# Operands' taps and steps on three rotating PSUM banks, and the last image's 3x3 convolution by pairs of rows

## The chip, the cores and the metric

The kernel runs on one core of one Trainium2 chip, in one launch. The metric is the device time of an execution in microseconds (us); smaller is better. The engines are named as in the profile: PE is TensorE, whose weight loads are shown as PEld, DVE is VectorE, ACT is ScalarE, POOL is GpSimd, SP is SyncE. SP issues almost all DMA transfers, in the order in which its instructions stand.

## The reference

The input is x, 4 images of 128 channels by 64x64 pixels, in f32. Four layers follow each other, each with a residual and each behind a group norm `gn` of 32 groups:

```python
x = x + attention(gn(x), Wq, bq, Wk, bk, Wv, bv)   # 4096 tokens of 128 channels, softmax(q k / sqrt(128)) v
x = x + conv5x5(gn(x), radial kernel of 5x5 taps)
x = x + scan_layer(gn(x), ...)                     # see below
x = x + conv3x3(gn(x), main_w) + main_b
```

The scan layer applies a 1x1 convolution, and splits the 128 channels into two halves, of which the second runs over the pixels backwards. Each half gets a causal convolution of 4 taps and a silu (the result is `xt`), then `delta = softplus(xt @ Wd + bd)`, `Bm = xt @ WB` and `Cm = xt @ WC`, and for every channel and each of 64 states the recurrence

```python
h[t] = exp(delta[t] * A) * h[t-1] + delta[t] * xt[t] * Bm[t]
y[t] = sum over the states of h[t] * Cm[t] + D * xt[t]
```

A 1x1 convolution leads back to 128 channels. The other branch of the 3x3 layer's `where` gives the same value, so that only the 3x3 convolution itself is computed.

## The kernel before

**Three streams in one order of instructions.** An image is a tile of 128 channels by 4096 pixels in SBUF. A PSUM bank holds 128x512 f32, so that an image is 8 tiles of 512 pixels or 4 chunks of 1024 (16 rows of 64 pixels). The Python generators `images`, `front`, `attention_start`, `conv_pairs`, `scan_operands` and `back` emit instructions piece by piece, and the loop at the end of `program` interleaves them with `scan_core`, the recurrence. `scan_core` has 1024 ticks, 256 for each image; the image number is b. A tick is one pass over 128 rows (32 channels times 4 states) of 1024 pixels: a decay on ACT (L1075), a drive `db` on POOL (L1082), the scan on DVE (L1092), the product with Cm on DVE (L1095) or on POOL (L1113), and the sum over the states on PE (L1127). Each engine executes what it is given in that order. While the ticks of image b run, `front` works on image b+1: attention, the 5x5 convolution by pairs of rows (`conv_pairs`), then the operands of its own scan.

**The operands.** `scan_operands` makes delta, delta*xt, Bm and Cm of an image for `scan_core`. It walks in slots; tile i (0 to 7) starts at slot 5i. The steps of tile i, with their slots counted from its start, are

| slot | step | engine, line |
|---|---|---|
| 0, 1 | `taps`: 8 matmuls of half width (4 taps, two directions) into the bank `pt` | PE L887 |
| 4 | `halves`: half of `pt` to SBUF (`xc`), its tanh (for b > 0 in place, in `pt`) | ACT L901, L906 |
| 5 | `silu`: product of the two, into `xc` | DVE L910 |
| 8 | `delta_product`: matmul into the bank `pz` | PE L919 |
| 9, 12 | `row_product` of Bm and of Cm, both through the bank "a" | PE L919 |
| 10, 12 | `softplus`, `exp` on `pz` | ACT L932, L933, L959, L964 |
| 11, 13 | `row`: the two rows to SBUF, and from there to DRAM | ACT L924, SP L926 |
| 13 | `digits`: reads `pz` for the last time | DVE L938, L939 |

So PE meets, in each five slots, `taps(k)`, the second `row_product(k-2)`, `delta_product(k-1)`, the first `row_product(k-1)`, and then `taps(k+1)`. After tiles 3 and 7 (1, 5 and 7 in image 0) come the logarithms (ACT L968, with a table load before and after), `join` and `drives` on POOL (L944, L949) and the writes of delta and delta*xt. Before the first ticks of image b are emitted, `before(b)` draws out work until the first chunk of its operands is ready. `load` then brings the operands from DRAM for the ticks (L1052, L1058), on the SP queue.

All `pt` of an image use one bank, "s". A tile `pt(k+1)` can be written only when `pt(k)` has been read for the last time: by `silu(k)` for b > 0, by `halves(k)` for b = 0. The `pz` alternate between the banks "z" and "s2". The bank pool that holds "s2" is closed when the last image's operands are done, and its space becomes two double-width tiles "da" (`widen`).

**The end.** After the last tick, `scan_end` and `group_norm` of image 3 run, and then `back(3)`, with nothing beside it. It calls `conv` (from L610 on): ACT writes the normalised image into a padded tile in four pieces (L370), and for each of the 8 tiles of 512 pixels PE accumulates 9 products (L644), one for each tap. `put` adds bias and image on DVE (L1278), and SP writes the tile out (L1279). For images 0 to 2 the image is added by a tenth matmul with the identity, and the tile leaves over ACT; that work lies among the ticks of image 3.

`program(True)` is a second version of everything, for inputs whose softmax leaves the safe range; it is not entered here. It reads its convolution weights back from the DRAM copy `kept`.

Of the kernel before, what the change touches and what calls it, by code (L numbers as in the profile page):

```python
# [24 lines left out]
F32 = mybir.dt.float32  # L25
I32 = mybir.dt.int32
AF = mybir.ActivationFunctionType
ALU = mybir.AluOpType
# [4 lines left out]
P = 128  # L33
GROUPS = 32
GN_EPS = 1e-5
CH = 1024
MM = 512
# [8 lines left out]
PRODUCT, HOP, SLOT, PACE, ENDPACE, AHEAD = 0.86, 1.7, 0.7, 2.8, 1.5, 4  # L46


BQ, BK, BX, BP, CONVB, BD, DSKIP, MAINB, CONVW, ALOG = 0, 1, 2, 3, 4, 5, 6, 7, 8, 12
# [3 lines left out]
def conv_preact_kernel(  # L53
# [16 lines left out]
    nc = tc.nc  # L70
    B, C, H, W = x.shape
    L = H * W
    NCH = L // CH
# [6 lines left out]
    NM = L // MM  # L80
# [4 lines left out]
    of = out.rearrange("b c h w -> b c (h w)")  # L85
# [3 lines left out]
    dram = ctx.enter_context(tc.tile_pool(name="dram", bufs=2, space=DRAM))  # L89
    ps = ctx.enter_context(tc.tile_pool(name="ps", bufs=1, space=PSUM))  # L90
    pools, ready = {}, set()
    more = None

    def bank(tag, name):
        return pools.get(tag, ps).tile([P, MM], F32, tag=tag, name=name)
# [32 lines left out]
    def col(i):  # L128
        return vec[:, i : i + 1]
# [93 lines left out]
    cw = const.tile([P, NTAP + 10, C], F32, name="cw")  # L223
    taps5 = cw[:, :NTAP, :]

    m3 = cw[:, : main_w.shape[1], :]
    kept = dram.tile([P, main_w.shape[1], C], F32, tag="kept", bufs=1, name="kept")

    def build_conv_weights(tmp):
        xx_sb = tmp.tile([P, NTAP, C], F32, name="xx_sb")  # L230
        nc.sync.dma_start(xx_sb, xhat)
        id_sb = tmp.tile([P, C], F32, name="id_sb")
        nc.sync.dma_start(id_sb, identity)
        picked = tmp.tile([P, 2, NTAP, C // 2], F32, name="picked")
        for n, (which, table, inds) in enumerate((("xx", wxx, indsxx), ("id", wid, indsid))):
            nr, oc = table.shape[1], table.shape[2]
            acc = picked[:, n]
            one = cw.rearrange("p k c -> p (k c)")[:, : NTAP * oc]
            one = one.rearrange("p (k o) -> p k o", o=oc)
            tab = tmp.tile([P, nr, oc], F32, name=f"tab{which}")  # L240
            nc.sync.dma_start(tab, table)
            ii = tmp.tile([P, NTAP], I32, name=f"ii{which}")
            nc.sync.dma_start(ii, inds.to_broadcast([P, NTAP]))
            fi = tmp.tile([P, NTAP], F32, name=f"fi{which}")
            nc.vector.tensor_copy(fi, ii)

            ng = tmp.tile([P, NTAP], F32, name=f"ng{which}")
            nc.vector.tensor_scalar(ng, fi, 0.0, float(nr), ALU.is_lt, ALU.mult)
            nc.vector.tensor_tensor(fi, fi, ng, ALU.add)
            nc.vector.tensor_scalar(fi, fi, 0.0, float(nr - 1), ALU.max, ALU.min)  # L250
            for r in range(nr):
                hit = tmp.tile([P, NTAP], F32, name=f"hit{which}{r}")
                nc.vector.tensor_scalar(hit, fi, float(r), None, ALU.is_equal)
                hit_b = hit.unsqueeze(2).to_broadcast([P, NTAP, oc])
                tab_b = tab[:, r : r + 1, :].to_broadcast([P, NTAP, oc])
                if r == 0:
                    nc.vector.tensor_tensor(acc, tab_b, hit_b, ALU.mult)
                else:
                    nc.vector.tensor_tensor(one, tab_b, hit_b, ALU.mult)
                    nc.vector.tensor_tensor(acc, acc, one, ALU.add)  # L260
                yield HOP

        for t in range(2):
            def every(ap):
                return ap.rearrange("p k (o t) -> p k o t", t=2)[:, :NTAP, :, t]

            idb = id_sb.rearrange("p (o t) -> p o t", t=2)[:, :, t].unsqueeze(1)
            idb = idb.to_broadcast([P, NTAP, C // 2])
            nc.vector.tensor_tensor(every(xx_sb), every(xx_sb), picked[:, 0], ALU.mult)
            nc.vector.tensor_tensor(every(cw), picked[:, 1], idb, ALU.mult)  # L270
            yield HOP
        nc.vector.tensor_tensor(taps5, taps5, xx_sb, ALU.add)
        for n in range(2):
            row = cw[:, (1 + 2 * n) * 5 :]
            nc.vector.tensor_tensor(
                cw[:, NTAP + n * 5 : NTAP + (n + 1) * 5, :], row[:, :5], row[:, 5:10], ALU.add
            )
        nc.sync.dma_start(kept, m3)

# [1 line left out]
    ASIZE, VSIZE = HP * (W + PAD) + PAD, (H + 2) * (W + 2) + PAD  # L283
# [85 lines left out]
    def normalise(dst, src, gn):  # L369
        nc.scalar.activation(dst, src, AF.Identity, scale=gn[0], bias=gn[1])  # L370
# [292 lines left out]

# [198 lines left out]
    def scan_operands(b, xn, mats4, piece):  # L867


        bc, dd, dxd, xcd, xsd = mats4  # L870
        pad = KC - 1

        xc = large(b, f"xc_{b}")[:, :L]
        delta = pools["big"].tile([P, L], F32, tag="xt", name=f"delta_{b}")
        pts, ths, pzs, pbs, us = {}, {}, {}, {}, {}

        def taps(i, *ks):
            if ks[0] == 0:
                pts[i] = bank("s", f"pt_{b}_{i}")
            pt = pts[i]  # L880
            t = i * MM
            for k in ks:
                lo = L + 2 * pad - 1 - k - t - (MM - 1)
                views = (xn[:, t + k : t + k + MM], xn[:, lo : lo + MM][:, ::-1])
                for d, view in enumerate(views):
                    r = slice(d * HALF, (d + 1) * HALF)
                    nc.tensor.matmul(  # L887
                        pt[r, :], wtap[:, k, r], view,
                        start=k == 0, stop=k == KC - 1,
                        tile_position=(0, d * HALF), skip_group_check=True,  # L890
                    )
                    if i == 0 and k == 0:
                        nc.tensor.matmul(
                            pt[r, : pad], ident[:, r], edge, start=False, stop=False,
                            tile_position=(0, d * HALF), skip_group_check=True,
                        )
# [20 lines left out]
        def product(i, m, tag):  # L917
            pb = bank(tag, f"pb{m}_{b}_{i}")
            nc.tensor.matmul(pb, bdiag[:, m, :], xc[:, bass.ts(i, MM)], start=True, stop=True)  # L919
            return pb  # L920
# [29 lines left out]
            nc.sync.dma_start(dxd[c], xc[:, cut])  # L950

        def delta_product(i):
            pzs[i] = product(i, 0, ("z", "s2")[i % 2])

        def row_product(i, m):
            pbs[i, m] = product(i, m, "a")
# [9 lines left out]
        def logs(i, j):  # L966
            for n in range(i, j):
                nc.scalar.activation(us[n], us[n], AF.Ln)  # L968

        slots = {}  # L970

        def at(slot, f, *args):
            slots.setdefault(slot, []).append((f, args))

        EVERY = 5
        for i in range(NM):
            t = EVERY * i
            at(t, taps, i, 0, 1)
# [14 lines left out]
        for i, j in zip(cuts, cuts[1:]):  # L993
            t = EVERY * (j - 1) + 15
            at(t, logs, i, j)
# [203 lines left out]
    def program(safe):  # L1199
# [1 line left out]
        mats4, ynds, ends = {}, {}, {}  # L1201
        ready.clear()
        if safe:
            nc.sync.dma_start(m3, kept)

        def load(tile, b):
            for c in range(NCH):
# [15 lines left out]
        def front(b, xn, v):  # L1223

            xs = large(b + 1, f"xs_{b}")[:, :L]
            st = Sums(f"e{b}")
            yield from attention(b, xs, xn, v, st, safe, load(xs, b))
            st2 = Sums(f"s{b}")

            yield from conv_pairs(b, xs, f"A{b % 2}", st, st2, b > 0 or safe)  # L1230
            if b + 1 == B:
                nc.sync.dma_start(m3, main_w)

            def mat(name):
                return dram.tile([NCH, P, CH], F32, tag=name, name=f"{name}_{b}")

            mats4[b] = (
                [mat("bm"), mat("cm")], mat("dd"), mat("dxd"), mat("xcd"),
                dram.tile([P, L], F32, tag="xsd", bufs=B, name=f"xsd_{b}"),
            )  # L1240
            ynds[b] = dram.tile([NM, P, MM], F32, tag="ynd", bufs=B, name=f"ynd_{b}")
            operands = yield from scan_prep(b, xs, st2, mats4[b])
            if b + 1 < B:
                return (yield from both(operands, start(b + 1, 10)))
            yield from operands

        def stage(b, pieces, done):

# [19 lines left out]
        def back(b):  # L1268
            xs, st, _ = ends[b]

            def put(i, acc):
                cut = bass.ts(i, MM)
                if b + 1 < B:
                    to = pools["bg"].tile([P, MM], F32, tag="w", bufs=4, name=f"o_{b}_{i}")
                    nc.scalar.activation(to, acc, AF.Identity, bias=col(MAINB))
                else:
                    to = xs[:, cut]
                    nc.vector.scalar_tensor_tensor(to, acc, col(MAINB), to, ALU.add, ALU.add)  # L1278
                nc.sync.dma_start(of[b][:, cut], to)  # L1279

            yield from conv(b, xs, "V", st, m3, 3, put, "m", residual=b + 1 < B)

        def both(*gens):

# [174 lines left out]
```

## Time and profile before

| what | us |
|---|---|
| median of 3 runs (4513.7 to 4527.3) | 4513.8 |
| the profiled execution, its own time | 4519.1 |
| its span, first to last instruction | 4517.3 |
| busy in the span: PE | 3996.2 |
| busy: DVE | 3667.9 |
| busy: POOL | 3638.5 |
| busy: ACT | 2399.5 |
| operands of image 0, from the first `taps` to the last | 643.0 to 694.3 |
| operands of image 1, the same | 1585.9 to 1654.8 |
| operands of image 2, the same | 2542.7 to 2617.2 |
| operands of image 3, the same | 3505.5 to 3568.9 |
| the last image's 3x3 convolution, matmuls | 4444.0 to 4508.7 |

Every f32 matmul shows as two records of the profile. "L887" is line 887 of the kernel. In a timeline, the bracket at the end of a row gives the idle time of that engine just before the instruction, and what ended it. Waits are a list of who waited for whom: us in total, how often, and the longest.

### The profile page before, as it was taken

To read this page: it belongs to the slowest core of one execution; us is meant where nothing else is said; L and a number is where in the kernel's file an instruction comes from. 1 tells how busy PE (TensorE), PEld (TensorE's weight loads), DVE (VectorE), ACT (ScalarE), POOL (GpSimd) and SP (SyncE) were. 2 spreads that over 40 slices of the span, in tenths; PEclk is the share of its full clock that TensorE was granted. 3 is DMA by queue.
4 is the path that set the end of the run, shared out by engine and by line. 5 is a ranking of instruction groups with operands and counts; after the bars stand their busy time and mean duration, and the time that the engine had idled before them with its cause. 6 is when DMAs were issued, how large, how long until landed. Compare 5 with 4: busy or idle time off the path is not lost. (4 is left out here: it accounts for less than half of the span.)

```text
span 4517.3 us, 43608 instructions
## 1 busy us (share of the span) xinstructions
PE 3996.2 (88%) x13528; PEld 1482.2 (33%) x13528; DVE 3667.9 (81%) x3643; ACT 2399.5 (53%) x4420; POOL 3638.5 (81%) x1731
## 2 busy tenths in 40 slices
PE   8999998999999979999999879999999658575767
PEld 4444433333333323333333223333333112121212
DVE  4721217999998978999989879999999799999992
ACT  3333227666664476666654566666654654544441
POOL 3433308999998969999989789999999899999992
PEclk9999999999999989999999989999999878697888
DMA  1000016445444565455445555455445565656561
GB/s 63 6 1 1 5 60 229 171 168 180 170 175 157 174 218 196 172 179 174 174 154 177 188 209 176 162 176 177 175 161 182 211 226 203 233 193 231 184 233 48
DMA packets 210582, 719.51 MB, mean 159 GB/s; under 512 B 24864, under 2 KB 25760, under 8 KB 210208
## 3 DMA queue, kind: packets, MB, share of 16 engines
q1 hardware_dynamic: 208736, 715.87, 44.8%
q8 instruction: 109, 1.79, 0.2%
q14 instruction: 137, 1.12, 0.1%
q10 hardware_dynamic: 1600, 0.73, 0.1%
HBM read 649.07 MB, written 67.44 MB: 159 GB/s over the span
## 5 line engine op out<-in xcount | busy, mean ns | idle before, releaser
L1082 POOL TENSOR_TENSOR db<-dx,br 128x1024 f32<-128x1024 f32 x1024 | 2400.0, 2367 | 226.9 <-DMA dx<-dxd 76.7
L1075 ACT ACTIVATE da<-de,a_neg 128x512 f32<-128x512 f32 (+1 forms) x1795 | 1342.1, 751 | 736.0 <-DVE da L1092 444.5
L465 PE MATMUL sc<-r,x 128*128 128x512 f32 x2048 | 1082.5, 611 | 18.3 <-ACT r L434 12.4
L477 PE MATMUL acc<-pt,v 128*128 128x512 f32 x2048 | 1046.5, 593 | 1.6
L1113 POOL TENSOR_TENSOR hc<-hc,cr 128x1024 f32<-128x1024 f32 x406 | 960.1, 2365 | 17.6 <-ACT last L1108 15.1
L471 ACT ACTIVATE pt<-sc 128x512 f32<-128x512 f32 x1024 | 604.4, 590 | 572.4 <-PE sc L465 563.9
L1127 PE MATMUL y<-hc,sel 128*32 128x512 f32 x4096 | 654.2, 650 | 276.6 <-POOL hc L1113 273.5
L1095 DVE TENSOR_TENSOR hc<-da,cr 128x512 f32<-128x512 f32 (+1 forms) x1067 | 828.4, 776 | 68.8 <-issue 1.3
L1092 DVE TENSOR_TENSOR_SCAN da<-da,last,db 128x512 f32<-128x512 f32 (+1 forms) x464 | 728.1, 1569 | 24.1 <-POOL db L1082 17.6
L1092 DVE TENSOR_TENSOR_SCAN da<-da,da,db 128x512 f32<-128x512 f32 x449 | 577.9, 1287 | 14.3 <-ACT da L1075 13.4
L465 PEld LDWEIGHTS sc<-r,x 128*128 128x128 f32 x2048 | 359.1, 190 | 605.0 <-issue 378.4
L477 PEld LDWEIGHTS acc<-pt,v 128*128 128x128 f32 x2048 | 387.5, 190 | 497.2 <-issue 477.9
L1092 DVE TENSOR_TENSOR_SCAN hc<-da,hc,db 128x512 f32<-128x512 f32 x322 | 413.2, 1283 | 61.9 <-ACT da L1075 31.6
L1092 DVE TENSOR_TENSOR_SCAN hc<-da,last,db 128x512 f32<-128x512 f32 (+1 forms) x304 | 455.9, 1500 | 8.4 <-ACT da L1075 4.7
L519 POOL TENSOR_TENSOR sidep<-sidep,pt 128x512 f32<-128x512 f32 x120 | 170.5, 1421 | 279.9 <-ACT pt L471 277.8
L1127 PEld LDWEIGHTS y<-hc,sel 128*32 128x32 f32 x4096 | 94.1, 111 | 732.3 <-POOL hc L1113 363.6
L644 PE MATMUL pcm<-xpm,cw 128*128 128x512 f32 x576 | 291.2, 653 | 30.5 <-ACT xpm L370 30.5
L519 DVE TENSOR_TENSOR sided<-sided,pt 128x512 f32<-128x512 f32 x120 | 96.0, 800 | 227.5 <-ACT pt L471 226.1
L1092 DVE TENSOR_TENSOR_SCAN da<-da,db 128x512 f32<-128x512 f32 (+1 forms) x154 | 231.0, 1500 | 30.9 <-ACT da L1075 16.2
L808 PE MATMUL pe<-df,cw 128*128 128x512 f32 x560 | 255.2, 598 | 0.0
L499 PE MATMUL zp<-pt,ones 128*32 128x512 f32 x1536 | 202.4, 595 | 5.0 <-DVE xs L563 5.0
L1108 ACT COPY last<-da 128x1 f32<-128x1 f32 x469 | 73.1, 156 | 244.3 <-DVE hc L1095 242.5
(209 smaller groups left out, 2743.2 us busy)
## 6 DMA issues: line engine op xcount, KB each, us to landing
br<-bm SPq DMA_DIRECT2D x512, 512.0 KB, 5.2
cr<-cm SPq DMA_DIRECT2D x512, 512.0 KB, 3.9
de<-dd SPq DMA_DIRECT2D x64, 512.0 KB, 4.8
dx<-dxd SPq DMA_DIRECT2D x64, 512.0 KB, 6.2
x<-in_x_dram SPq DMA_DIRECT2D x16, 512.0 KB, 4.6
xs<-in_x_dram SPq DMA_DIRECT2D x16, 512.0 KB, 5.8
xsd<-xs SPq DMA_DIRECT2D x16, 512.0 KB, 5.2
xcd<-xc SPq DMA_DIRECT2D x16, 512.0 KB, 2.7
```

The costliest lines, as they stand in the source:

```text
L465: nc.tensor.matmul(sc, xn[:, bass.ts(j, P)], rq[blk], start=True, stop=True)
L471: nc.scalar.activation(pt, sc, AF.Exp)
L477: nc.tensor.matmul(acc[blk], v[:, j, :], ring[:, u % NRING, :], start=j == 0, stop=j == NJT - 1)
L519: eng.tensor_tensor(s, s, ring[:, u % NRING, :], ALU.add)
L644: nc.tensor.matmul(acc.rearrange("p (r w) -> p r w", w=W), weights[:, t, :], xp[:, y : y + RPM, dx : dx + W], start=t == 0, stop=t == k * ...
L808: nc.tensor.matmul(flat(acc), cw[:, w * K5 + dx, :] if w < HSUM else more[:, w - HSUM, dx, :], view(r, dx), start=k == 1, stop=k == total ...
L1075: nc.scalar.activation(da, rep["de", b, c, d, g][:, bass.ts(h, size)], AF.Exp, scale=a_neg[:, at(i)])
L1082: nc.gpsimd.tensor_tensor(dbs[i], rep["dx", b, c, d, g], rows["b", b, c, d, q], ALU.mult)
L1092: nc.vector.tensor_tensor_scan(h, da, db[:, cut], before, ALU.mult, ALU.add)
L1095: nc.vector.tensor_tensor(hc[:, cut], h, rows["c", b, c, d, q][:, cut], ALU.mult)
L1113: nc.gpsimd.tensor_tensor(hcs[i], hcs[i], rows["c", b, c, d, q], ALU.mult)
L1127: nc.tensor.matmul(y[r : r + SG, :], sel, hcs[i - KG + 1 + gg][:, bass.ts(h, MM)], start=q == 0, stop=False, tile_position=(0, r), skip_gr ...
```

## The change

1. In `scan_operands`, the `pt` and the `pz` of an image are put in one list in the order of their slots (`pt(i)` at 5i, `pz(i)` at 5i + 8), and take the banks "s", "z", "s2" in turn along it. The last `pz` takes "z". The slots and the order of the instructions on every engine stay.
2. The last image's 3x3 convolution becomes `conv_last`. For a pair of output rows it needs the rows d0 to d3; it forms d2-d1 and d3-d1 on POOL and d1+d2 and d0-d2 on DVE (`combine`), multiplies each of the four by three taps, and gets both rows from the four sums. A chunk of 16 rows takes 12 matmuls into four banks (odd chunks the banks s, a, z, y; even chunks the two tiles "da"). The difference part leaves over ACT (`nc.scalar.copy`) and is added and subtracted on POOL; DVE adds the other three parts and the bias. One DMA writes a chunk.
3. `last_weights` makes the six combined taps that this needs, on DVE, when the last image's operands have been emitted. `kept` grows from 9 to 15 taps.

```diff
+    LSUM, LDIF, NKEPT = 9, 12, 15
+    kept = dram.tile([P, NKEPT, C], F32, tag="kept", bufs=1, name="kept")
...
+    def last_weights():
+        half, above = cw[:, LSUM : LSUM + 3, :], cw[:, LDIF : LDIF + 3, :]
+        nc.vector.tensor_tensor(half, m3[:, 0:3, :], m3[:, 6:9, :], ALU.add)
+        nc.vector.tensor_scalar(half, half, 0.5, None, ALU.mult)
+        nc.vector.scalar_tensor_tensor(above, m3[:, 3:6, :], -0.5, half, ALU.mult, ALU.add)
+        nc.vector.scalar_tensor_tensor(half, m3[:, 3:6, :], 0.5, half, ALU.mult, ALU.add)
+
+    def conv_last(b, xs, st, finish):
+        CK = CH // W // 2
+        xp = pools["big"].tile([P, VSIZE], F32, tag="V", name=f"xpl_{b}")
+        rows = xp[:, : (H + 2) * W].rearrange("p (h w) -> p h w", w=W)
+        nc.gpsimd.memset(rows[:, 0, :], 0.0)
+        nc.gpsimd.memset(rows[:, H + 1, :], 0.0)
+        gn = yield from group_norm(st, f"m{b}")
...
+        def piece(c):
+            h0, h1 = 2 * CK * c + (c > 0), min(2 * CK * (c + 1) + 1, H)
+            normalise(rows[:, 1 + h0 : 1 + h1, :], xh[:, h0:h1, :], gn)
...
+        def combine(c):
+            d = [rows[:, 2 * CK * c + k : 2 * CK * (c + 1) + k - 1 : 2, :] for k in range(4)]
+            made = []
+            for eng, pairs in (
+                (nc.gpsimd, ((2, 1, ALU.subtract), (3, 1, ALU.subtract))),
+                (nc.vector, ((1, 2, ALU.add), (0, 2, ALU.subtract))),
+            ):
+                two = pools["hc"].tile([P, CH], F32, tag="hc", name=f"cb_{b}_{c}_{len(made)}")
+                for n, (i, j, op) in enumerate(pairs):
+                    made.append(flat(two[:, bass.ts(n, MM)]))
+                    eng.tensor_tensor(made[-1], d[i], d[j], op)
+            combined[c] = made
+
+        def banks_of(c):
+            if c % 2:
+                return [bank(tag, f"pl{tag}_{b}_{c}") for tag in "sazy"]
+            two = [
+                pools["wide"].tile([P, CH], F32, tag="da", bufs=2, name=f"pl{n}_{b}_{c}")
+                for n in range(2)
+            ]
+            return [t[:, bass.ts(h, MM)] for t in two for h in range(2)]
+
+        def products(acc, view, w):
+            for n, dx in enumerate((1, 0, 2)):
+                to = slice(max(1 - dx, 0), W - max(dx - 1, 0))
+                of_ = slice(max(dx - 1, 0), W - max(1 - dx, 0))
+                nc.tensor.matmul(
+                    flat(acc)[:, :, to], cw[:, w + dx, :], view[:, :, of_],
+                    start=n == 0, stop=n == 2, skip_group_check=True,
+                )
...
+        piece(0)
+        combine(0)
+        piece(1)
+        combine(1)
+        for c in range(NCH):
+            t_, o_, s_, e_ = banks_of(c)
+            diff, odd, total, even = combined.pop(c)
+            products(t_, diff, LDIF)
+            products(s_, total, LSUM)
+            products(e_, even, 0)
+            products(o_, odd, 6)
+            if c + 2 < NCH:
+                piece(c + 2)
+                combine(c + 2)
+            ts_ = pools["bg"].tile([P, MM], F32, tag="w", bufs=4, name=f"t_{b}_{c}")
+            nc.scalar.copy(ts_, t_)
+            nc.gpsimd.tensor_tensor(part(c, 0), part(c, 0), flat(ts_), ALU.add)
+            nc.gpsimd.tensor_tensor(part(c, 1), part(c, 1), flat(ts_), ALU.subtract)
+            for y, own in enumerate((e_, o_)):
+                nc.vector.scalar_tensor_tensor(
+                    part(c, y), flat(s_), col(MAINB), part(c, y), ALU.add, ALU.add
+                )
+            for y, own in enumerate((e_, o_)):
+                nc.vector.tensor_tensor(part(c, y), flat(own), part(c, y), ALU.add)
+            finish(c)
+            yield HOP
...
         def taps(i, *ks):
             if ks[0] == 0:
-                pts[i] = bank("s", f"pt_{b}_{i}")
+                pts[i] = bank(ring["pt", i], f"pt_{b}_{i}")
...
         def delta_product(i):
-            pzs[i] = product(i, 0, ("z", "s2")[i % 2])
+            pzs[i] = product(i, 0, ring["pz", i])
...
+        order = sorted([(EVERY * i, "pt", i) for i in range(NM)] + [(EVERY * i + 8, "pz", i) for i in range(NM)])
+        ring = {(what, i): ("s", "z", "s2")[n % 3] for n, (_, what, i) in enumerate(order)}
+        ring["pz", NM - 1] = "z"
...
             yield from operands
+            last_weights()
...
-            yield from conv(b, xs, "V", st, m3, 3, put, "m", residual=b + 1 < B)
+            if b + 1 < B:
+                yield from conv(b, xs, "V", st, m3, 3, put, "m", residual=True)
+            else:
+                yield from conv_last(
+                    b, xs, st,
+                    lambda c: nc.sync.dma_start(of[b][:, bass.ts(c, CH)], xs[:, bass.ts(c, CH)]),
+                )
```

More of the change, by code (lines that the diff above doesn't have):

```diff
@@ L226, in conv_preact_kernel @@
     m3 = cw[:, : main_w.shape[1], :]
-    kept = dram.tile([P, main_w.shape[1], C], F32, tag="kept", bufs=1, name="kept")
+    LSUM, LDIF, NKEPT = 9, 12, 15
+    kept = dram.tile([P, NKEPT, C], F32, tag="kept", bufs=1, name="kept")
     def build_conv_weights(tmp):
@@ L277, in build_conv_weights @@
             )
-        nc.sync.dma_start(kept, m3)
+        nc.sync.dma_start(kept, cw[:, :NKEPT, :])
     ASIZE, VSIZE = HP * (W + PAD) + PAD, (H + 2) * (W + 2) + PAD
@@ L658, in conv, with flat, part @@
         finish(*done)
+    def last_weights():
[11 more added lines that the diff above has]
+        gn = yield from group_norm(st, f"m{b}")
+        xh = xs.rearrange("p (h w) -> p h w", w=W)
+        def flat(t):
+            return t.rearrange("p (h w) -> p h w", w=W)
+        def piece(c):
+            h0, h1 = 2 * CK * c + (c > 0), min(2 * CK * (c + 1) + 1, H)
+            normalise(rows[:, 1 + h0 : 1 + h1, :], xh[:, h0:h1, :], gn)
+        combined = {}
+        def combine(c):
[26 more added lines that the diff above has]
+                )
+        def part(c, y):
+            return xs[:, bass.ts(c, CH)].rearrange("p (h t w) -> p h t w", t=2, w=W)[:, :, y, :]
+        piece(0)
[24 more added lines that the diff above has]
+            yield HOP
@@ L871, in scan_operands @@
         pad = KC - 1
+        EVERY = 5
         xc = large(b, f"xc_{b}")[:, :L]
@@ L973, in at @@
             slots.setdefault(slot, []).append((f, args))
-        EVERY = 5
         for i in range(NM):
@@ L1203, in program @@
         if safe:
-            nc.sync.dma_start(m3, kept)
+            nc.sync.dma_start(cw[:, :NKEPT, :], kept)
         def load(tile, b):
@@ L1272, in put @@
                 cut = bass.ts(i, MM)
[L1273 to L1278, printed above, removed]
-                nc.sync.dma_start(of[b][:, cut], to)
-            yield from conv(b, xs, "V", st, m3, 3, put, "m", residual=b + 1 < B)
+                to = pools["bg"].tile([P, MM], F32, tag="w", bufs=4, name=f"o_{b}_{i}")
+                nc.scalar.activation(to, acc, AF.Identity, bias=col(MAINB))
+                nc.sync.dma_start(of[b][:, cut], to)
+            if b + 1 < B:
[5 more added lines that the diff above has]
+                )
         def both(*gens):
```

## The prediction

> **What bounds the kernel now.** I read the page first: DVE (81% of the span) and POOL (81%) share the scan with PE (88%), and no engine bounds every stage. So I went by the two stages that the change touches. The chain of waits that ended last, over the end of the kernel:
>
> ```profile
> 4442.70 1.25 ACT xpm L370
> 4443.95 0.04 issue
> 4444.00 64.67 PE pcm L644 x144
> 4508.69 0.75 DVE xt L1278
> ```
>
> One engine alone: 72 products (144 records) after one normalised piece, then one DVE operation. The rest of the profiled execution, 4509.4 to 4517.3, is the branch on the safe range and the closing of the program.
>
> For the operands, who waited for whom, asked for each of the four operand stages in turn (images 0, 1, 2, 3; us, times, longest):
>
> ```profile
> PE pt L887 <- ACT th L906: 1.4, 1, 1.4
> PE pt L887 <- DVE xc L910: 12.8, 5, 6.7
> PE pt L887 <- DVE xc L910: 16.6, 6, 11.2
> PE pt L887 <- DVE xc L910: 6.3, 5, 1.4
> ```
>
> PE stands idle ahead of `taps` until `silu` (or, in image 0, the tanh) has read bank "s". The timelines of three engines in image 1 show one round:
>
> ```profile
> 1615.54 0.66 ACT L906 ACTIVATE pt<-pt,hbias 128x512 f32<-128x512 f32 x1
> 1616.23 0.69 DVE L910 SCALAR_TENSOR_TENSOR xc<-pt,xc 128x512 f32<-128x512 f32 x1 [1.44 <-ACT pt L906]
> 1616.98 3.66 PE L887 MATMUL pt<-xn,wtap 128*64 128x512 f32 x16 [1.35 <-DVE xc L910]
> ```
>
> Taps follow each other at 1600.3, 1609.1, 1617.0, 1624.5 and 1632.4, 8.0 us apart, where PE has 3.66 of taps, 2.93 of products and about 1 of the ticks' sums. ACT idles in turn for what stands behind the taps on PE (1.46 to 3.04 us each time before the row copy L924). PE is therefore the bound of this round, with idle time in it. The long gaps come at the last `taps`. In image 2, on PE, ACT, SP, SP and POOL:
>
> ```profile
> 2611.00 6.25 PE L887 MATMUL pt<-xn,wtap 128*64 128x512 f32 x16 [11.23 <-DVE xc L910]
> 2619.33 0.59 ACT L924 COPY bs<-pb 128x512 f32<-128x512 f32 x1 [6.10 <-PE pb L919]
> 2619.95 0.32 SPq L926 DMA_DIRECT2D cm<-bs  x1
> 2621.54 0.60 SPq L1058 DMA_DIRECT2D br<-bm  x1
> 2629.06 2.36 POOL L1082 TENSOR_TENSOR db<-dx,br 128x1024 f32<-128x1024 f32 x1 [11.11 <-DMA br<-bm]
> ```
>
> This is one chain: a late `silu` holds the taps, the row product behind them, the row copy, the row's write, the loads of the next ticks that stand behind this write on SP, and POOL for 11.11 us. Image 1 has the same (gap 6.68 before 1648.75, Cm write at 1656.55, loads behind it, POOL idle 8.12 before 1664.09).
>
> **What the Trainium skill says.** "PSUM — Partial Sum Buffer", in its summary of rules, wants a reader and a running matmul on different banks; the gaps above are that wait on "s". "DMA: Bandwidth & Descriptors", in the anatomy of one DMA, says that a semaphore wait happens on the issuing sequencer, not in the DMA engines; the trace agrees, the loads leave 0.4 us and more after the row write that had waited. "TensorE: Matmul & The Clock Gate", "What's actually happening", has PE at half clock until some 3.4 us of activity; here the last convolution's weight loads stand 0.86 us apart until 4449.3 and 0.43 after. The same page's engine queues are strict FIFO for ACT, DVE and GpSimd, as the late `silu` behind ticks' scans shows.
>
> **Part 1, the banks.** Along the list, `pt(k+1)` takes the bank of `pz(k-2)`, so it waits for `digits(k-2)` instead of `silu(k)`. Both are on DVE and `digits(k-2)` is two slots earlier in its order, so this wait can't end later than the old one. `pz(k-1)` takes the bank of `pt(k-1)`, free after `silu(k-1)`, whose result it multiplies anyway. `pt1` meets a bank idle since the convolution. "s" and "s2" come free for the next image's attention no later than before. So a loss is excluded for the bank waits, and no instruction is added or moved past another. What goes is the idle before taps, tile by tile from the timeline of PE:
> - image 0: 1.36 (tile 1). Later tiles show none: 3.66 + 2.93 = 6.59 is already the distance, 6.56. Sum 1.4.
> - image 1: 2.06 + 1.33 + 1.35 + 1.35 (tiles 1, 3, 4, 6) = 6.1, all ahead of the logarithms, so the whole stage moves up. Then tile 7: `digits(4)` ended its read at 1640.2, PE is free at 1642.1, so its taps end at about 1645.8, not 1654.8; the row product follows, the row copy waits its turn on ACT to about 1647, and the loads leave about 8.5 earlier. POOL's idle of 8.12 goes; I count 8.1. Sum 14.2.
> - image 2: 2.06 + 1.35 + 1.01 + 0.74 = 5.2. Tile 7 could start at 2600, but the second row product needs the copy of the first, which ACT does at 2610.8 (it waits 8.06 for a scan, which stays). So the second copy comes at 2613.2 instead of 2619.33: 6.1 of POOL's 11.11. Sum 11.3.
> - image 3: 1.06 + 1.35 + 1.22 + 1.35 + 1.35 = 6.3.
>
> Together 33.2. Next late in a round are the products' wait for bank "a" (about 0.35 each, it stays) and the tables of the logarithms. After the stage the ticks run as before, only earlier, and the following stages with them. Some of the idle will turn up there again; I take seven eighths, 29. Bounds: 8 (only half of the short gaps is gained, 19.0 / 2, less 1.5 lost to new collisions), and 42 (all, and the half-clock taps of 6.1 and 6.25 us become 3.66, with rounds that shed the 0.35).
>
> **Part 2, the last convolution.** Removed: 72 products by 0.858 (two records, 0.429 apart) = 61.8, plus 2.9 of the half clock = 64.7, as the chain has it. Added: 48 by 0.858 = 41.2, less 0.4 (two of three products have 63 of 64 columns), plus the same 2.9 = 43.7. Ahead of the first product stands now POOL's subtraction. The pair convolution of before has its like, and the matmuls behind it:
>
> ```profile
> L713 POOL TENSOR_TENSOR df<-xpe 128x528 f32<-128x528 f32 x12 | 14.4, 1200 | 0.0
> L731 DVE TENSOR_TENSOR combos<-xpe 128x528 f32<-128x528 f32 x12 | 11.4, 1008 | 2.2 <-ACT xpe L370 2.2
> L808 PE MATMUL pe<-df,cw 128*128 128x512 f32 x560 | 255.2, 598 | 0.0
> ```
>
> That is +1.2, with a longer first piece and a semaphore +1.3. The end keeps one DVE operation (0.68 against 0.75). A chunk costs PE 12 by 0.858 = 10.3; POOL 4 by 1.2 to 1.27 = 5; DVE 2 by 1.0 and 4 by 0.7 = 4.8; ACT 1.3 + 0.6. PE covers them all, with six "hc" buffers for three chunks ahead. In the last chunk the copy of t starts 9 products (7.7) before the end, POOL needs 2.5, DVE 1.5, all done before the last sum. If this cover were gone, the 10 us of one chunk's other work would show at its end. The last write is 512 KB instead of 256: by the DMA page's fit 0.6 longer, an estimate, under PE's branch of 4.67 us at the end: nothing. Net 43.7 + 1.3 - 64.7 = -19.7; bounds -22 (no start cost, and less half clock) and -10 (products wait for combinations about 2.4 us a chunk).
>
> **Part 3, small things.** Four DVE operations of 384 elements, 0.5 to 1.1 each by L1095's 0.69 for 512 and L731's slower ones: 2 to 4.4 us, behind image 3's operands, where DVE is busy 4.48 of 10 us (3600 to 3610) and POOL's ticks hide them; +0.5. Without that cover, 4. `kept` is written 0.4 MB larger in the first image, when the DMA share is near nothing: 0.
>
> **Sum**: -29 - 19.7 + 0.5 = -48. The profiled execution would go from 4519.1 to 4471 (span 4469); it lies 5.3 over the median, so the median goes from 4513.8 to 4466. A measurement of this kernel tells some 0.3%, 13.5 us, from no change.
>
> **Rivals.**
> - *The wait moves* (14%). The taps start earlier, but the round is then bound by ACT, the row bank "a" and the loads of the ticks, and the gaps come back there. For it: ACT is at 9.8 of 10 us in 1630 to 1640, and POOL waits 76.7 for dx and 41.8 for br over the run. Against: ACT's own idle is mostly for PE. Ring worth 5: 4513.8 - 5 - 19.7 + 0.5 = 4490.
> - *The last convolution is fed too slowly* (7%): combinations wait for pieces, or PE for combinations, and half the gain is left, -10: 4513.8 - 29 - 10 = 4475.
> - *Chunks that don't overlap* (2%), ending slower. If a bank or buffer holds chunk c+1 until chunk c is evicted, PE falls back to half clock each time: piece 1.3, POOL 2.4, 12 products by 1.72 = 20.6, copy 0.6, POOL 2.5, DVE 2.9, together 30.3, by 4 = 121 against 66: +55, with the banks' 29 about 4540. It decides from an idle and half-clock loss of (19.7 + 29 + 13.5) / 4 = 15.5 us a chunk. Against it: L808's idle 0.0 in the same pattern.
> - *It doesn't do what it says* (3%): the waits stay under another name in both stages, 4513.
>
> **How the numbers follow.** The forecast holds with 74%, its own range 4455 to 4478. The rivals lie at 4490, 4475, 4540 and 4513. The range takes the bounds of both parts: 4513.8 - 42 - 22 = 4450, and 4513.8 - 8 - 19.7 = 4486. Above it lie half or more of the first rival and the last two, somewhat under 2 in 10. Faster by over 0.3%: the forecast, the first two rivals: 0.95; same 0.03; slower 0.02.
>
> **What would show it.** Right: the wait of L887 for L910 near zero; taps of images 1 to 3 about 7 us apart; Cm's late write in image 1 and 2 gone and POOL's two long DMA idles (8.12, 11.11) at most half; the last convolution in 96 records over 43 to 44 us without gaps, starting 2.6 us after the norm. Wrong: idle before L924, L919 or L1082 grows by what L887 loses, or the last convolution shows gaps over 3 us and half-clock loads in its later chunks.

## The result, and the profile after

The changed kernel takes 4472.73 us (median of 4 runs, 4471.1 to 4477.01), the kernel before on the same chip 4517.09 (4513.7 to 4527.3). The ratio is 0.9899, with a 95% interval of 0.9883 to 0.9915: about 44 us faster, where the prediction had 48 and a range of 28 to 64. The profiled execution took 4477.01, its span is 4475.2.

To see where the 44 us were gained I cut each span at the first `taps` of the images, at the last group norm and at the end. In such a stage two profiles of the changed kernel differ by up to 3.3 us (image 2: 950.6 and 953.9).

| stage (us) | before | after | difference | prediction |
|---|---|---|---|---|
| first `taps` of image 0 to those of image 1 | 942.9 | 941.8 | -1.1 | -1.4 |
| image 1 to image 2 | 956.8 | 948.6 | -8.2 | -14.2 |
| image 2 to image 3 | 962.8 | 950.6 | -12.2 | -11.3 |
| image 3 to the last norm | 937.0 | 935.0 | -2.0 | -6.3 + 0.5 |
| last norm to the end | 74.8 | 54.6 | -20.2 | -19.7 |

The prediction took one eighth off the four bank terms, for idle time that turns up again.

The end of the kernel, in the chain that ended last (start, duration, what):

```profile
4420.57 0.19 POOL nb_m L367
4420.76 1.37 issue
4422.16 1.79 POOL cb L704
4423.95 0.04 issue
4423.99 12.67 PE pl L721 x24
...
4457.05 2.55 PE pls L721 x6
4459.60 2.55 PE plz L721 x6
4462.15 2.55 PE ply L721 x6
4464.70 2.56 PE pla L721 x6
4467.28 0.69 DVE xt L752
```

The 96 records run from 4423.99 to 4467.26, 43.3 us against 64.67, with nothing between them. The first 24 hold all of the half clock (12.67 against 10.19 for the later 24). One POOL operation stands ahead of them, one DVE operation behind them.

Who waited for whom on PE in the operand stages (us in total, times, longest). Image 1, 1590 to 1657:

```profile
PE pb L1016 <- ACT bs L1021: 6.2, 3, 2.8
PE pb L1016 <- DVE xc L1007: 2.1, 1, 2.1
```

Image 2, 2530 to 2640:

```profile
PE pb L1016 <- ACT bs L1021: 12.9, 4, 7.1
PE pt L984 <- ACT xn L372: 10.7, 1, 10.7
```

`taps` is now L984 and `silu` L1007. The line of L984 waiting for L1007 is gone; what is left for L984 is the wait of each image's first tile for the normalised input, which the kernel before had too. The wait for the copy of a row out of bank "a" (L1021, before L924) has grown: from 1.9 to 6.2 us in image 1 and from 4.2 to 12.9 in image 2. The timeline of PE shows the rounds of image 1:

```profile
1607.23 3.66 PE L984 MATMUL pt<-xn,wtap 128*64 128x512 f32 x16
...
1613.67 3.66 PE L984 MATMUL pt<-xn,wtap 128*64 128x512 f32 x16
...
1621.22 3.66 PE L984 MATMUL pt<-xn,wtap 128*64 128x512 f32 x16
```

They start 6.4 to 7.6 us apart, 7.0 on average, against 8.0, and no bracket gives an idle time before them.

### The profile page after: what moved, and what is told of

Same layout as the page of the kernel before. It is cut to its first block, busy times and chain, and to the rows that moved or that the text cites. A ratio compares the mean times of both kernels' runs of the same rounds, so it can differ in the third digit from the quotient of the medians.

```text
span 4475.2 us, 43573 instructions
## 1 busy us (share of the span) xinstructions
PE 3978.4 (89%) x13480; PEld 1478.5 (33%) x13480; DVE 3693.8 (83%) x3663; ACT 2401.4 (54%) x4424; POOL 3661.3 (82%) x1745
## 5 line engine op out<-in xcount | busy, mean ns | idle before, releaser
L1176 ACT ACTIVATE da<-de,a_neg 128x512 f32<-128x512 f32 (+1 forms) x1795 | 1342.0, 751 | 740.5 <-DVE da L1193 449.5
L646 PE MATMUL pcm<-xpm,cw 128*128 128x512 f32 x432 | 226.0, 666 | 24.5 <-ACT xpm L372 24.5
```

The lines of the kernel that those rows point to most:

```text
L646: nc.tensor.matmul(acc.rearrange("p (r w) -> p r w", w=W), weights[:, t, :], xp[:, y : y + RPM, dx : dx + W], start=t == 0, stop=t == k * ...
L1176: nc.scalar.activation(da, rep["de", b, c, d, g][:, bass.ts(h, size)], AF.Exp, scale=a_neg[:, at(i)])
```

## The experiments

My theory at this point: the change is two independent gains. The banks save the idle of PE ahead of `taps`, most of it where it delays the ticks (POOL); the convolution saves its 24 products. The rivals were that one part had done it all, that only the wait of the last tile counted, and, for what fell short (image 1 and image 3), that the wait had moved, or that a small added part cost more than I had counted.

### The change again

No edit: the changed kernel in one batch with the next three.

> The changed kernel again, beside the others on one chip, as their measure. Both theories: 40 to 45 us under the kernel before (ratio 0.990 to 0.991).

Measured 4477.9 (4 runs) against 4521.27, ratio 0.9901 (0.9886 to 0.9916): 43.4 us. The result repeats.

### Each part alone

```diff
 kernel before, with the new ring alone
-                pts[i] = bank("s", f"pt_{b}_{i}")
+                pts[i] = bank(ring["pt", i], f"pt_{b}_{i}")
...
-            pzs[i] = product(i, 0, ("z", "s2")[i % 2])
+            pzs[i] = product(i, 0, ring["pz", i])
```

> The kernel before with the rotating banks alone; old last convolution, no combined taps. My theory, that the gaps ahead of the taps are the gain and that the combined taps then cost about 4 us in image 3's scan: 1 + 8 + 12 + 6 = 27 us under the kernel before, and first taps of image 3 and last norm 20 and 26 us earlier than in the kernel before. Rival, that what image 3's stage loses again comes from the loads behind the stage and not from the combined taps: 22 us under the kernel before, with the ticks 768 to 798 losing 4 us again as in the changed kernel.

The other half is the changed kernel with these two lines put back, so that it has `conv_last` and `last_weights` alone.

> The changed kernel with the old banks: pair convolution and combined taps alone. My theory, parts independent: -20.2 for the convolution, +4 for the combined taps, so 16 us under the kernel before. Rival, that the combined taps cost nothing: 20 us under it. If the two parts needed each other, this and the banks alone would not sum to the changed kernel's gain of 42.

Banks alone: 4491.92 (5 runs), ratio 0.9936 (0.9923 to 0.9950), 29.4 us. Convolution alone: 4504.78 (6 runs), ratio 0.9967 (0.9955 to 0.9979), 16.5 us. Their sum is 45.9, the whole 43.4: within the intervals the parts add up, and neither did it all. With the banks alone the first taps of image 3 and the last norm come 18.3 and 24.5 us earlier, where 20 and 26 were expected. The stages say more than the sums. With the banks alone, image 3 takes 930.8 us up to the last norm, 6.2 less than before (the prediction had 6.3). With the convolution alone it takes 940.4, 3.4 more than before, although nothing but `last_weights` is added there. In the changed kernel, with both, it takes 935.0, 4.2 more than with the banks alone. So the added weights cost some 4 us, where the prediction had counted 0.5. The rival, that the loads behind the stage take back what image 3 gains, fails: with the banks alone they don't.

### What the combined taps cost

The timeline of DVE in the changed kernel shows why:

```profile
3574.20 0.69 DVE L1196 TENSOR_TENSOR hc<-da,cr 128x512 f32<-128x512 f32 x1
3574.81 2.49 DVE L670 TENSOR_TENSOR cw<-cw 128x384 f32<-128x384 f32 x1
3577.34 2.45 DVE L671 TENSOR_SCALAR cw<-cw 128x384 f32<-128x384 f32 x1
3579.82 2.65 DVE L672 SCALAR_TENSOR_TENSOR cw<-cw 128x384 f32<-128x384 f32 x1
3582.50 2.58 DVE L673 SCALAR_TENSOR_TENSOR cw<-cw 128x384 f32<-128x384 f32 x1
```

Four operations of 384 elements take 10.2 us, 2.5 each, while the scan's product of 512 elements just ahead of them took 0.69. POOL, at the same time:

```profile
3576.85 5.20 POOL L1046 TENSOR_TENSOR xc<-delta,xc 128x1024 f32<-128x1024 f32 x2
3581.99 2.67 POOL L1183 TENSOR_TENSOR db<-dx,br 128x1024 f32<-128x1024 f32 x1
...
3594.83 4.66 POOL L1183 TENSOR_TENSOR db<-dx,br 128x1024 f32<-128x1024 f32 x2 [2.16 <-DVE da L1193]
```

Each of the four lasts about as long as the POOL operation beside it. And POOL, which was to hide them, runs into the delayed scans: it stands idle for 2.16 us for a DVE scan. The Trainium skill has this on the page "SBUF — State Buffer", in "Who interferes with whom": a DVE instruction with two inputs in SBUF contends with a GpSimd instruction that reads SBUF, and `tensor_scalar` can enter a mode that does; one with at most one SBUF input outside such modes does not. The trace agrees: the three with two SBUF inputs and the `tensor_scalar` take as long as POOL's operations beside them, and the scan's products, which read one operand from PSUM, keep 0.69 beside POOL. The mode itself shows in no trace here. To test it I moved the four operations to where POOL is done:

```diff
             yield from operands
-            last_weights()
...
             else:
+                last_weights()
                 yield from conv_last(
```

> The changed kernel with the four operations of the combined taps moved from behind image 3's operands to after the last tick, where DVE waits 9.7 us for the last norm's sums and POOL is idle. My theory: the four take 0.4 to 0.6 us each there instead of about 2.5, all hidden, and the kernel is 4 us faster than the changed one. Rival, that the loads behind the stage set the pace of ticks 770 to 776: the same time as the changed kernel within 1 us.

Measured 4471.32 (4 runs), ratio 0.9893 (0.9878 to 0.9908), against 4477.9 for the changed kernel in the same batch. The intervals of the two ratios overlap, so the 6.6 us between the medians are not settled by the times. The traces are clearer. Here is DVE with the late taps:

```profile
4399.12 0.55 DVE L670 TENSOR_TENSOR cw<-cw 128x384 f32<-128x384 f32 x1
4399.70 0.36 DVE L671 TENSOR_SCALAR cw<-cw 128x384 f32<-128x384 f32 x1
4400.10 0.56 DVE L672 SCALAR_TENSOR_TENSOR cw<-cw 128x384 f32<-128x384 f32 x1
4400.69 0.56 DVE L673 SCALAR_TENSOR_TENSOR cw<-cw 128x384 f32<-128x384 f32 x1
4408.67 0.17 DVE L323 TENSOR_REDUCE gn_sums<-su_m 128x2 f32<-128x16 f32 x1 [7.43 <-ACT junk L316]
```

2.0 us instead of 10.2 for the same four operations, in a place where DVE waits 7.43 us anyway. Image 3 then takes 929.6 us, as with no weights at all (930.8). In the five profiles with the late taps (this one and four below) the stage takes 927.4 to 933.6, on average 929.5, in the two with the early ones and the new banks 935.0 and 935.1. So the rival fails and the cost is shown, but its size only roughly: the three comparisons give 3.4, 4.2 and 5.5 us.

### Which waits carry the banks' gain

The kernel before, with only the last tile in another bank:

```diff
+        ring = {("pt", i): "s" for i in range(NM)}
+        ring.update({("pz", i): ("z", "s2")[i % 2] for i in range(NM)})
+        ring["pt", NM - 1], ring["pz", NM - 2], ring["pz", NM - 1] = "z", "s2", "z"
```

> The kernel before, with one tile of eight moved: only the last taps of each image go to bank z (the last two steps to s2 and z), all others stay on s. My theory, that the late taps of tile 7 hold the loads of the next ticks in images 1 and 2 and that the short gaps are a gain of their own: from the first taps of one image to those of the next about 4.5 us less for image 1 and 6 less for image 2, 1 less for image 3, so 11 us under the kernel before, against 29 with all banks rotating. Rival, that the short gaps of tiles 1 to 6 lie under other work and nearly all the gain is tile 7: 24 us or more under the kernel before.

Measured 4509.15 (10 runs) against 4519.34, ratio 0.9978 (0.9969 to 0.9987): 10.2 us, as the theory had it in total. The idle ahead of the last tile's taps is gone from its timeline, and the short gaps (2.05, 1.32, 1.35 and 1.35 us in image 1) stand as before. By stages it is less clear: image 1 gained 2.5 and image 2 9.2, where I had expected 4.5 and 6, and image 3 took 0.9 more instead of 1 less. So the rival, that nearly all the gain is the last tile, fails. About a third of the banks' 29.4 us comes from the last tiles. The other two thirds are a difference of medians, 19.2 us; that they come from the short gaps, which add up to 19.0 in the prediction, is argued and not measured one by one.

Is it the rotation that counts, or only that consecutive taps have different banks? With taps in "s" and "z" in turn and all steps in "s2":

```diff
+        ring = {("pt", i): ("s", "z")[i % 2] for i in range(NM)}
+        ring.update({("pz", i): "s2" for i in range(NM)})
+        ring["pz", NM - 1] = "z"
```

> The kernel before with another use of the same three banks: taps alternate between s and z, the steps all stay on s2 (the last on z). Now a step's matmul waits for the last reading of the step before it, which stands in the same slot. My theory, that what counts is that each bank's last reader comes well ahead in the order of its new writer: taps find their bank free, but the steps' matmul waits for the digits of the tile before, on DVE behind scans, so part of the gain is lost: 15 to 24 us under the kernel before. Rival, that any second bank for the taps gives the whole gain: 29 us under it, as with the rotating banks.

Measured 4499.93 (5 runs), ratio 0.9957 (0.9943 to 0.9970), 19.4 us, within the theory's 15 to 24. In image 1 the waits of PE (1580 to 1670) show the new limit:

```profile
PE pb L920 <- DVE delta L940: 9.1, 4, 3.8
```

With one bank for all steps, `delta_product` waits for `digits` of the tile before it. With the ring alone there is no such line; the largest there, apart from the first tile's, is 6.2 us in all for the row copy. Yet images 1, 2 and 3 take 950.2, 949.6 and 932.0 us, as with the ring (949.7, 951.4, 930.8). Only image 0 is 3.7 longer, and the intervals of the two ratios overlap. Inconclusive: the wait is there, but whether it costs time is not shown.

### Why image 1 gained less than predicted

In image 1, counted from its first taps, POOL meets the ticks after the operands 8.3 us earlier than before (1656.26 against 1664.09, with the first taps 0.4 later), where the prediction had 14.2. It splits into two. POOL's idle ahead of it fell from 8.12 to 3.56, that is 4.6 of 8.1. And its work before this idle was done 3.7 earlier, of the 6.1 that the short gaps were to give. SP's timeline and POOL's show what is late now:

```profile
1644.85 0.38 SPq L1023 DMA_DIRECT2D cm<-bs  x1
1649.33 0.53 SPq L1153 DMA_DIRECT2D de<-dd  x1
1649.94 0.56 SPq L1153 DMA_DIRECT2D dx<-dxd  x1
...
1656.26 2.36 POOL L1183 TENSOR_TENSOR db<-dx,br 128x1024 f32<-128x1024 f32 x1 [3.56 <-DMA dx<-dxd]
```

The row's write (L1023), which left at 1656.55 before, leaves at 1644.85 now, nearly 12 us earlier. But the load of dx behind it leaves only 7.8 us earlier, at 1649.94 instead of 1657.76. SP waited between them, in the waits of 1640 to 1660:

```profile
SPq L1153 <- ACT da L1176: 4.1, 1, 4.1
```

Loads of delta go round three buffers, and the last decay (L1176) that reads the oldest of them has yet to run. The wait for the row copy (8.4 us on SP in the same stretch of the kernel before) hid this one. A fourth buffer takes it away. Its memory comes from "hc", which goes from six buffers to five, so that step has a kernel of its own. Both have the late taps.

```diff
 first
-tc.tile_pool(name=f"hc{safe}", bufs=6)
+tc.tile_pool(name=f"hc{safe}", bufs=5)
...
 then also
-                    t = pools["rep"].tile([P, CH], F32, tag=name, name=f"{name}_{b}_{c}_{d}_{g}")
+                    t = pools["rep"].tile(
+                        [P, CH], F32, tag=name, bufs=4 if name == "de" else 3, name=f"{name}_{b}_{c}_{d}_{g}"
+                    )
```

> The combined taps late, and five buffers instead of six for hc. It makes the SBUF space for the next run and is its measure. Both theories: as the run with the taps late, or some us slower by waits of DVE and POOL for hc.

> As the run before with five hc buffers, and four buffers instead of three for de. In the changed kernel the first loads of image 1's ticks wait 4.1 us on SP for the last decay that reads the old de buffer, where before they waited 8.4 for the row copy. My theory, that this wait has taken the place of half of the one removed: it goes, POOL's wait for dx there (3.6 to 3.9) falls under 1, and image 1's stage is 3 to 4 us shorter than with five hc buffers alone. Rival, that POOL is held there by the time that the transfers take (dx lands 6 us after its issue) or by the next load: the same within 1 us.

Five "hc" buffers: 4471.82, ratio 0.9893 (0.9878 to 0.9908), the same as with six. With four buffers for delta: 4466.07, ratio 0.9885 (0.9870 to 0.9900). In image 1 of the latter, the wait of that load (now L1155) for the decay is gone. The timelines of SP and POOL:

```profile
1644.29 0.38 SPq L1023 DMA_DIRECT2D cm<-bs  x1
1644.71 0.53 SPq L1155 DMA_DIRECT2D de<-dd  x1
1645.33 0.73 SPq L1155 DMA_DIRECT2D dx<-dxd  x1
...
1654.07 2.35 POOL L1185 TENSOR_TENSOR db<-dx,br 128x1024 f32<-128x1024 f32 x1 [1.93 <-DMA dx<-dxd]
```

POOL's wait for dx falls from 3.2 us (with five "hc" buffers and three for delta) to 1.9, not under 1. The load of dx leaves 4.5 us earlier (1645.33 against 1649.79), but it takes 8.6 us to land, against 5.8: the core's DMA engines are busy 80 to 98% of the time from 1640 to 1660 (in steps of 5 us), and seven other transfers left in the 4.4 us before it. So the buffer did hold the loads, and with that wait gone the time of the transfers holds POOL, which is the rival's cause. What the buffer costs the kernel is open. There are 5.8 us between the medians, with intervals that overlap, and POOL's idle in image 1 makes up 1.3 of them. Image 1's stage takes 945.0 us against 950.9 with five "hc" buffers, but with six, and three for delta, it took 946.2 too.

### Start of the last convolution, and everything together

PE's first product comes 3.2 us after the norm's last value, since ACT's first piece takes 1.3 and POOL's first difference 1.79. With the late taps, and the first chunk's combinations all on DVE:

```diff
-                (nc.gpsimd, ((2, 1, ALU.subtract), (3, 1, ALU.subtract))),
+                (nc.gpsimd if c else nc.vector, ((2, 1, ALU.subtract), (3, 1, ALU.subtract))),
```

> The combined taps late as in the run before, and the first chunk's four combinations all on DVE. In the changed kernel POOL's first difference takes 1.78 us beside DVE's sums, and PE starts 3.2 us after the norm. My theory: DVE alone makes the difference in 0.7, PE starts 2.1 us after the norm, last norm to end 1.1 us shorter (53.0 instead of 54.1); no difference that the rounds can tell. Rival, that DVE's four in a row then hold the third and fourth group of products: PE gets a gap in the first chunk and nothing is won.

Its chain at the same place:

```profile
4412.45 1.30 ACT xpl L372
4413.78 0.70 DVE cb L704
4414.48 0.04 issue
4414.52 13.12 PE pl L721 x24
```

The first product comes 2.1 us after the norm, 1.1 sooner, as expected. But the first 24 records take 13.12 us, against 12.67 in the changed kernel and 12.35 with the late taps, with no gap between them: six weight loads at the start stand 0.84 us or more apart, where with the late taps there are four. From the norm to the end it is 53.6 us against 54.1. The time, 4469.05 (4 runs, ratio 0.9893, 0.9878 to 0.9908), doesn't resolve so little.

Late taps, four delta buffers and the first chunk on DVE together:

> The changed kernel with all that the runs point to: combined taps late, first chunk's combinations on DVE, five hc and four de buffers. My theory: image 1's and image 3's stages as in the run with four de buffers, last norm to end 53.6: 10 to 12 us faster than the changed kernel, ratio to the kernel before about 0.988. Rival, that the four de buffers' gain over five hc buffers was scatter between profiles: as the run with the combined taps late, 0.9893.

4466.03 (4 runs) against 4519.3, ratio 0.9881 (0.9866 to 0.9896). The median is 53 us under the kernel before, and not to be told from that of the run with four delta buffers (4466.07). Nor does the interval rule out the rival's 0.9893. Image 1's stage takes 947.0 us, image 3's 927.4, and from the last norm to the end it is 54.1, not the 53.6 expected: the earlier start has not shown a gain twice. It is about 10 us under the changed kernel if the two gains over the kernel before are compared (53.3 and 43.4); the two were not run side by side, and the intervals of their ratios overlap.

## Why the prediction was right, and where not

**The banks, image 0 (1.4).** -1.1 in the changed kernel, -1.2 with the banks alone: within the scatter of a stage, so not shown either way. The argument that no bank wait can end later holds for the other images only: in image 0 the old wait was for the tanh on ACT, not for DVE.

**Image 1 (14.2).** Measured 8.2. Two terms were too large. "POOL's idle of 8.12 goes; I count 8.1": it fell by 4.6, because I followed the loads back to the row write and stopped there, and didn't ask what SP meets next. It is the wait of 4.1 for the old delta buffer, and behind it the time of the transfers, which left POOL 1.9 of idle when there was a fourth buffer. The sum of short gaps, "6.1, all ahead of the logarithms, so the whole stage moves up", gave 3.7. From the first taps to those of tile 6, PE is 5.2 ahead (41.3 us against 46.5). Right behind them its two waits for bank "a" take 3.3 instead of 1.9. That is the first rival's mechanism, "The wait moves", and it took part of one stage, not most of the gain.

**Image 2 (11.3).** Measured 12.2. "6.1 of POOL's 11.11" left 4.86 of it, so 6.25. The timelines of PE, SP and POOL:

```profile
2598.97 4.51 PE L1016 MATMUL pb<-xc,bdiag 128*128 128x512 f32 x6 [7.12 <-ACT bs L1021]
...
2601.69 0.32 SPq L1023 DMA_DIRECT2D cm<-bs  x1
...
2603.29 0.60 SPq L1159 DMA_DIRECT2D br<-bm  x1
...
2610.33 2.36 POOL L1183 TENSOR_TENSOR db<-dx,br 128x1024 f32<-128x1024 f32 x1 [4.86 <-DMA br<-bm]
```

As the prediction had it, the second row product now waits for the copy of the first (7.12 us), which has its own delay on ACT. ACT waits for a scan of DVE (8.11 us, 8.06 before), and the `silu` of the 11.23 us gap stood behind the same scans. I had overlooked what made them late. It is in the timelines of the kernel before, of DVE, POOL and ACT:

```profile
2601.32 1.18 DVE L354 TENSOR_TENSOR gn_work<-gn_work 128x32 f32<-128x32 f32 x1
2602.53 2.26 DVE L355 TENSOR_TENSOR gn_work<-gn_work 128x32 f32<-128x32 f32 x1
2604.83 2.26 DVE L356 TENSOR_TENSOR gn_work<-gn_work 128x32 f32<-128x32 f32 x1
...
2599.97 2.48 POOL L944 TENSOR_TENSOR delta<-delta,u 128x512 f32<-128x512 f32 x2
2602.41 4.63 POOL L949 TENSOR_TENSOR xc<-delta,xc 128x1024 f32<-128x1024 f32 x2
...
2609.01 0.69 ACT L1075 ACTIVATE da<-de,a_neg 128x512 f32<-128x512 f32 x1 [8.06 <-DVE hc L1092]
```

Three group-norm operations of 32 elements take 5.7 us beside POOL's `join` and `drives`; in the last norm, where POOL rests, they take 0.19 each. In the changed kernel they still take 1.20, 2.28 and 2.26. No run here moves them.

**Image 3 (6.3).** 6.2 with the banks alone. In the changed kernel 2.0, for the reason below.

**Seven eighths of the sum, 29.** The banks alone measured 29.4 us by the medians, and 25.8 by the stages of one profile (1.2, 7.1, 11.3, 6.2). The discount was a fair guess of the size of the loss, but it was not spread over the stages: nearly all of it sits in image 1.

**The last convolution (-19.7).** Measured -20.2. Products 43.3 (43.7 predicted). The start costs 1.9 more than before (3.2 us from the norm instead of 1.3) where I had 1.3: POOL's first difference took 1.79, not 1.2, since DVE's sums ran beside it. At the end some 0.7 less than before: there is one DVE operation, as predicted, and the writes of 512 KB took 2.6 us to land instead of 2.0 for 256 KB, the 0.6 of the estimate; the last one left at 4468.0 and landed before the end. The chunks overlap, as that rival had to deny, and nothing feeds PE late, although the combinations took longer than predicted. In the groups of the last convolution (4423 to 4468):

```profile
L704 POOL TENSOR_TENSOR cb<-xpl 128x512 f32<-128x512 f32 x8 | 12.6, 1610 | 1.4 <-ACT xpl L372 1.4
L704 DVE TENSOR_TENSOR cb<-xpl 128x512 f32<-128x512 f32 x7 | 11.2, 1659 | 0.0
```

1.66 on DVE where "DVE 2 by 1.0" stood, and 1.61 on POOL. A chunk of 10.2 us of products covers them. In the last chunk ACT's copy of the difference part ran 7.6 us before the last product ended (7.7 predicted); in the even chunks it came only after all 12 products, which cost nothing.

**The combined taps (+0.5).** This step failed: "POOL's ticks hide them; +0.5. Without that cover, 4". POOL's ticks are what makes them slow, 10.2 us of DVE instead of 2.0, and the scans behind them then hold POOL. I had a hint in L731's mean of 1008 ns against 692 for L1095, and read it as a longer operation, not as contention. Its median is 705 and its longest 1634: the mean mixes operations alone and beside POOL. The cost is 3.4 to 5.5 us.

**The sum.** Without the discount the terms were 52.4. By the stages, image 1 gave 6.0 less, image 3 with the weights 3.8 less and image 0 0.3 less, image 2 and the last convolution 0.9 and 0.5 more: 43.7. The discount had allowed for 4.2 of these 8.7, and the rest is the distance of the result from 48, within the forecast's own range.

## What to carry to other kernels

Give out accumulator banks in the order in which their last readers stand on their engines: here that took waits away without an instruction more, and by difference the many waits of about one microsecond were worth twice the few long ones. That the order matters, and not just a second bank for the taps, is not shown. When a transfer is late, follow the issuing queue one wait further than the one that shows, since the next buffer's wait may stand right behind it, and ask how long the transfer takes if it leaves sooner. Going by the combined taps, small elementwise work with SBUF inputs goes to a time when GpSimd rests, not beside GpSimd work that is thought to hide it.

## What the hardware showed that I had not expected

DVE operations of 384 elements with both inputs in SBUF took 2.49, 2.65 and 2.58 us beside POOL's products, and 0.55 to 0.56 alone; the one with a single SBUF input and a constant took 2.45 and 0.36. The size hardly counted: operations of 32 elements took 2.26 beside POOL's products of 1024 in image 2, and 0.19 alone. It goes both ways: POOL's differences of 512 elements took 1.61 on average beside DVE's sums (in the pair convolution of before, L713, the median is 1.13 and the longest 1.60), and these 1.66 instead of the 0.70 of the version in which POOL rested. The scan's products with an operand in PSUM kept 0.69 throughout.
